# Layer 0 of a four-layer network: prelude in emitted order, its keys and first operand rows copied out of SBUF, transfers moved from GpSimd's queue to SyncE's

## The chip, the cores and the metric

One core of a Trainium2 chip runs the whole network in one launch. The metric is device time in microseconds (us); the times of several executions are given with their median. All data are float32. The core's engines are called as in the profile: PE (matrix multiplies), PEld (its weight loads), DVE (vector), ACT (scalar and activations), POOL (GpSimd), SP (which here only starts transfers, or DMAs). Each engine works through its own instructions in order, and one that waits holds up those behind it. DMAs can be started from SP, ACT or POOL.

## The reference

Four layers on an image of 2 x 64 x 64 positions with 128 channels. The change touches only layer 0, which is self-attention over the 4096 positions of each image with 4 heads of 32 channels and a learned relative bias in both directions:

```
x = x + L0(groupnorm(x))
q, k, v = split(x @ w_qkv)                    # 4 heads of 32
scores  = (q . k) / sqrt(32) + bias_w + bias_h   # [2, 4, 4096, 4096]
bias_w[query (x,y), key (a,b)] = q . pos_emb_w[b - y + 63]
bias_h[query (x,y), key (a,b)] = q . pos_emb_h[a - x + 63]
out     = softmax(scores) @ v
```

Layers 1 to 3 (a triangular product, an attention with a routed mixture of experts, and another such pair) follow it; their program does not change.

## The kernel before, in words

**Units, blocks and steps.** Layer 0 (function `layer0`) works on four *units*: image b and pair of heads p, in the order (0,0), (0,1), (1,0), (1,1). A unit has 8 *blocks* of 512 queries (`qb`), a block 4 *steps* (`xb`) of 1024 keys. So there are 32 blocks and 128 steps, written out in one loop by hand.

**A step.** For eight key tiles, PE makes scores `l0sc` (L766; four matmuls of 64 x 64 weights each, for two heads) into one of three PSUM buffers; ACT takes the exponential into an SBUF tile `l0es` (L774); DVE adds the tile into the running sum of the denominators `l0acc` (L777, L779). Then come a *piece* of side work (see below), and 32 matmuls `l0o` (L795) of the exponentials with the values. A step with `xb` 3 takes a second piece behind `l0o`.

**The bias inside the product.** A score matmul has 64 rows per head: 32 of q and k, 16 of the bias in one direction and 16 of that in the other. The keys' side is a tile `ka` (one for each pair p) whose lower rows hold keys and whose upper rows are constant one-hot rows, written on POOL by `l0_onehot` (L330). The queries' side is a tile `l0mv`, of which there are two, taken in turn by `xb % 2`. Function `fill` loads it over SP's queue: queries out of DRAM tensor `l0qd` (L629), rows of one bias out of `l0wd` (L632), rows of the other out of `l0hd` (L637). `prefill(at + 2)` at the end of a step starts the load for the step after the next one: 1 MB (`xb` 0 and 1, all three kinds), or 256 KB (`xb` 2 and 3, `l0hd` alone).

**How the bias rows are made** (`biases`, a generator of 17 pieces per unit). For each of 8 groups g: POOL turns the queries (`l0tq`, L567); PE multiplies them with the position table (`l0pw`, L539); ACT (or DVE) copies the result to a staging tile (`l0ew`, L550); two DMAs write it to DRAM (`l0sw`, L552); two DMAs read it back with a skewed pattern, which does the relative-to-absolute shift (`l0tw`, L586); POOL turns it back into its place (`l0rw`, L576). After eight groups four DMAs store `l0rw` as `l0wd` (L592). For the other direction (`l0ph`, `l0eh`, `l0sh`) the skewed read goes straight to `l0hd` (L598). The staging tile is one of the same ring of nine buffers as the exponentials (`tag="es", bufs=9`), so its DMA must have left it before its place is used again. `l0tw` has one buffer.

**Side work.** `side` is a list of generators, one piece of which is taken at each call of `piece()`: in unit 0 the rest of its own `biases`, those of unit 1, and the tokens (transposes and normalization) of image 1; in unit 1 the keys, values and queries of image 1 and the biases of unit 2; in unit 2 those of unit 3; in unit 3 none.

**Which queue.** Within the loop every DMA of the side work goes through `side_dma()`, which is POOL's queue there; SP's queue has only the fills and the copies of keys from DRAM into `ka` (`keys`, L615). Before the loop `side_dma()` is SP.

**End of a block.** While the next block runs: at its step 0 PE sums the denominators over partitions (`l0zb`, L700) and ACT copies them out; at step 1 DVE takes the reciprocal (L711) and POOL multiplies the numerators with it (`l0os`, L712); at step 2 PE folds the two halves (`l0po`, L717) and DVE adds the result to x (L728). `l0zb` and `l0po` share one PSUM buffer.

**Order.** The part ahead of the loop (the *prelude*: tokens, values, keys, queries of image 0, one-hot rows, and the first 11 pieces of unit 0's biases) is put in order by a scheduler. From `tc.manual_schedule()` on, which stands at the head of the loop, instructions are issued in the order in which the code emits them.

Of the kernel before, what the change touches and what calls it, by code (L numbers as in the profile page):

```python
# [14 lines left out]
P = 128  # L15
# [23 lines left out]
class Net:  # L39
# [239 lines left out]
    def l0_constants(self, wp, ap, ps, raw):  # L279

        nc = self.nc
        flip = ap.tile([P, 512], F32, tag="os", name="l0flip")[:, :P]
        nc.gpsimd.memset(flip, 0.0)
        nc.gpsimd.affine_select(
            out=flip,
            in_=flip,
            compare_op=ALU.not_equal,
            fill=1.0,
            base=2 - 2 * S,
            pattern=[[1, P]],  # L290
            channel_multiplier=1,
        )
        pos = wp.tile([P, 2, P], F32, tag="pos", name="l0pos")
        for i in range(2):
            pt = ps.tile([P, 512], F32, tag="misc", name=f"l0pe{i}")
            nc.tensor.matmul(
                pt[:, :P],
                lhsT=raw[:, i].rearrange("p h d -> p (h d)"),
                rhs=flip,
                start=True,  # L300
                stop=True,
            )
            nc.scalar.copy(pos[:, i, :], pt[:, :P])
        return pos
# [42 lines left out]
    def layer0(self):  # L347
# [7 lines left out]
        with ExitStack() as st:  # L355
            wp = st.enter_context(tc.tile_pool(name="l0w", bufs=1))
            ap = st.enter_context(tc.tile_pool(name="l0b", bufs=2))
            dp = st.enter_context(tc.tile_pool(name="l0d", bufs=1, space=DRAM))
            raw = self.l0_raw(ap)
            w = self.load(wp, "wqkv", [P, 3 * C], ins["L0_conv_w_qkv"])  # L360
# [12 lines left out]
            kd = [dp.tile([P, L], F32, tag=f"kd{b}", name=f"l0kd{b}") for b in range(B)]  # L373
# [9 lines left out]
            qTs, vs, rws = {}, {}, {}  # L383
# [12 lines left out]
            def side_dma():  # L396
                return nc.gpsimd if loop[0] else nc.sync

            def blocks(t, x):

                return t.rearrange("p (x a s k) -> p x s a k", x=NX, a=NX, s=2)[:, x]
# [10 lines left out]
            def tokens(ps, b):  # L412

                xT = ap.tile([P, L], F32, tag="xT", name=f"l0xT{b}", bufs=1)
                qTs[b] = xT
                st = self.small.tile([P, NC // 4, 6], F32, tag="gst", name=f"gst{b}", bufs=1)
                for x in range(NX):
                    pt = bank(ps, f"l0gt{b}_{x}")
                    for i in range(8):
                        nc.tensor.transpose(  # L420
                            pt[:, i // 4, i % 4 * P : (i % 4 + 1) * P],
                            self.x[:, b * NC + 8 * x + i, :],
                            self.ident,
                        )
                    for s in range(2):
                        nc.vector.bn_stats(st[:, 2 * x + s, :], pt[:, s, :])
                        nc.scalar.copy(
                            blocks(xT, x)[:, s].rearrange("p a (x y) -> p a x y", y=TB),
                            pt[:, s, :].rearrange("p (x a y) -> p a x y", a=NX, y=TB),
                        )  # L430
                    yield
                mv = self.small.tile([P, 2], F32, tag="gmv", name=f"gmv{b}")
                nc.vector.bn_aggr(mv, st)
                yield
                pm = bank(ps, f"gpm{b}")
                nc.tensor.matmul(
                    pm[:, 0, 0:1], lhsT=self.gmat, rhs=mv[:, 0:1], start=True, stop=True
                )
                gm = self.small.tile([P, 1], F32, tag="gm", name=f"gm{b}")
                nc.vector.tensor_copy(gm, pm[:, 0, 0:1])  # L440
                d = self.small.tile([P, 1], F32, tag="gd", name=f"gd{b}")
                nc.vector.tensor_tensor(d, mv[:, 0:1], gm, ALU.subtract)
                v = self.small.tile([P, 1], F32, tag="gv", name=f"gv{b}")
                nc.vector.scalar_tensor_tensor(v, d, d, mv[:, 1:2], ALU.mult, ALU.add)
                yield
                pv = bank(ps, f"gpv{b}")
                nc.tensor.matmul(pv[:, 0, 0:1], lhsT=self.gmat, rhs=v, start=True, stop=True)
                gr = self.small.tile([P, 1], F32, tag="gr", name=f"gr{b}")
                yield from self.rstd_parts(gr, pv[:, 0, 0:1], 1e-5, 1, apart=True)
                yield  # L450
                for x in range(NX):
                    part = xT[:, x * TB * S : (x + 1) * TB * S]
                    nc.vector.tensor_scalar(part, part, gm, gr, ALU.subtract, ALU.mult)
                    yield

            def project_v(ps, b):

                xT = qTs[b]
# [6 lines left out]
                for x in range(NX):  # L465
                    pv = bank(ps, f"l0pv{b}_{x}").rearrange("p s (i c) -> p (s i) c", c=C)
                    for i in range(8):
                        j = 8 * x + i
                        nc.tensor.matmul(
                            pv[:, i, :],  # L470
                            lhsT=xT[:, j * P : (j + 1) * P],
                            rhs=w[:, 2 * C :],
                            start=True,
                            stop=True,
                        )
# [9 lines left out]
            def project_k(ps, b):  # L485

                xT = qTs[b]
                for x in range(NX):
                    pk = bank(ps, f"l0pk{b}_{x}")
                    for s in range(2):  # L490
                        nc.tensor.matmul(
                            pk[:, s, :].rearrange("p (a k) -> p a k", k=P),
                            lhsT=w[:, C : 2 * C],
                            rhs=blocks(xT, x)[:, s],
                            start=True,
                            stop=True,
                        )
                    kst = staging(f"l0kst{b}_{x}")
                    nc.scalar.activation(kst, pk, AF.Copy, scale=root)
                    for s in range(2):  # L500
                        side_dma().dma_start(
                            out=blocks(kd[b], x)[:, s],
                            in_=kst[:, s, :].rearrange("p (a k) -> p a k", k=P),
                        )
                    yield

            def project_q(ps, b):

                xT = qTs[b]
                for x in range(NX):  # L510
                    pq = bank(ps, f"l0pq{b}_{x}")
                    for s in range(2):
# [3 lines left out]
                            rhs=blocks(xT, x)[:, s],  # L516
# [12 lines left out]
                    side_dma().dma_start(out=qd[b][:, cols], in_=xT[:, cols])  # L529
                    yield  # L530

            def slope(ps, u, n, g, tq):
# [16 lines left out]
                else:  # L549
                    nc.scalar.copy(ev[:LR], pt[:LR])  # L550
                for h in range(2):
                    side_dma().dma_start(  # L552
# [4 lines left out]
            def biases(hold, u):  # L557
# [15 lines left out]
                for k in range(2 * 8 + 1):  # L573
# [8 lines left out]
                    if 1 <= k < 9:  # L582
                        g = k - 1
                        tws[g] = ap.tile([P, 8, S], F32, tag="tw", name=f"l0tw{b}_{p}_{g}", bufs=1)
                        for h in range(2):
                            side_dma().dma_start(  # L586
# [3 lines left out]
                    if k == 9:  # L590
                        for c in range(0, L, L // 4):
                            side_dma().dma_start(  # L592
                                out=wd[u][:, c : c + L // 4], in_=rw[:, c : c + L // 4]
                            )
                    if k >= 9:
                        g = k - 9
                        for h in range(2):
                            side_dma().dma_start(  # L598
# [11 lines left out]
            def keys(u):  # L610
                b, p = u
                ka = kas[p]
                for h in range(2):
                    at = (2 * p + h) * HD
                    nc.sync.dma_start(  # L615
                        out=ka[64 * h : 64 * h + HD, :], in_=kd[b][at : at + HD, :]
# [6 lines left out]
            def fill(mv, u, qb, xb):  # L623
                b, p = u
                qs = slice(qb * 512, (qb + 1) * 512)
                for h in range(2):
                    at = (2 * p + h) * HD
                    if xb < 2:
                        nc.sync.dma_start(  # L629
                            out=mv[64 * h : 64 * h + HD], in_=wide(qd[b][at : at + HD, qs], HD)  # L630
                        )
                        nc.sync.dma_start(  # L632
                            out=mv[64 * h + 48 : 64 * h + 64],
                            in_=wd[u][:, qs].rearrange("(h s r) q -> h r s q", h=2, r=TB)[h],
                        )
# [6 lines left out]
            with tc.tile_pool(name="l0sp", bufs=2, space=PSUM) as ps:  # L642
# [3 lines left out]
                kas = self.l0_onehot(wp, ap, 2)  # L646
                for _ in project_v(ps, 0):
                    pass
# [4 lines left out]
                keys(units[0])  # L653
                hold = [ps]
                first[0] = biases(hold, units[0])
                for _ in range(11):
                    next(first[0])

            ps = st.enter_context(tc.tile_pool(name="l0p", bufs=1, space=PSUM))
            hold[0] = ps  # L660
            st.enter_context(tc.manual_schedule())
# [48 lines left out]
            def end_scale(e):  # L710
                nc.vector.reciprocal(e.r, e.r)  # L711
                nc.gpsimd.tensor_tensor(e.os, e.os, e.r, ALU.mult)  # L712
# [17 lines left out]
            mvs = [wp.tile([P, NX, 512], F32, tag=f"mv{i}", name=f"l0mv{i}") for i in range(2)]  # L730
# [10 lines left out]
            for at, (i, qb, xb) in enumerate(order):  # L741
# [3 lines left out]
                if (qb, xb) == (0, 1) and i == 0:  # L745
                    keys(units[1])
                if (qb, xb) == (7, 0) and i in (1, 2):
                    keys(units[i + 1])
# [33 lines left out]
                if prev:  # L782
# [4 lines left out]
                    elif xb == 2:  # L787
                        end_fold(prev)
# [16 lines left out]
            for part in (end_numerators, end_totals, end_scale, end_fold):  # L805
# [1292 lines left out]
```

## Time and profile before

| | |
|---|---|
| median of 3 runs | 4938.61 us (4929.92 to 4940.01) |
| the profiled execution | 4928.16 us |
| its span, first to last instruction | 4926.0 us |
| mean granted PE clock | 0.907 |
| first score matmul of the loop | 119.73 us after the start |
| last row of layer 0's end (addition to x) | about 1739 us |
| PE, DVE, ACT, POOL busy over the span | 88%, 62%, 48%, 20% |

The page of the profile gives each engine's busy time, the chain of work that ended last, and groups of instructions with their line, engine, count, mean time in ns and what ended the idle time before them. Besides, the trace can be asked for the waits in a stretch (who waited for whom, in total), for instructions in order of time ("start, duration, engine, line, ... [idle before <- what ended it]"), and for the busy time in stretches. POOLq and SPq are the queues' own instructions. The line numbers are those of the code above.

### The profile page before, as it was taken

What the parts mean: (1) busy time and instruction counts of PE and PEld (TensorE: products, weight loads), DVE (VectorE), ACT (ScalarE), POOL (GpSimd) and SP (SyncE); (2) the same over time, 40 slices, a digit from 0 to 9 for tenths busy, and PEclk for the clock granted to TensorE, in tenths of its full rate; (3) what the DMA queues carried; (4) which work ended last, traced back from release to release, by engine and by line L of the source; (5) the groups of instructions that cost most, each with busy time, mean ns of one, the idle gap of its engine ahead of it and who ended that gap; (6) DMA issues with size and microseconds to landing.
All of it is one profiled execution on the core that took longest, in us unless ns stands there. A gap on an engine that the chain in (4) does not pass through costs nothing.

```text
span 4926.0 us, 67757 instructions
## 1 busy us (share of the span) xinstructions
PE 4348.6 (88%) x27079; PEld 1851.4 (38%) x27079; DVE 3032.7 (62%) x4776; ACT 2377.9 (48%) x2850; POOL 991.0 (20%) x799
## 2 busy tenths in 40 slices
PE   4998999999999938488999999958999999999765
PEld 2222332323333326322332333328974444444432
DVE  2787887988999978646666565551043333333577
ACT  1666666666677614157777888820022222222200
POOL 4230023141000030134554555500020000000000
PEclk6999999999999958689999999965589999999889
DMA  5442334444333200000000000023300000000000
GB/s 161 97 112 56 73 81 106 85 108 84 66 58 63 46 8 1 25 1 1 1 1 1 1 1 1 1 71 103 103 2 0 0 0 0 0 0 0 6 13 22
DMA packets 150317, 192.25 MB, mean 39 GB/s; under 512 B 28996, under 2 KB 87204, under 8 KB 149602
## 3 DMA queue, kind: packets, MB, share of 16 engines
q1 hardware_dynamic: 113170, 130.34, 12.6%
q0 software_dynamic: 14912, 40.29, 2.8%
q10 hardware_dynamic: 21904, 17.12, 1.2%
q8 instruction: 218, 3.57, 0.3%
q14 instruction: 113, 0.93, 0.1%
HBM read 147.85 MB, written 48.23 MB: 40 GB/s over the span
## 4 chain that ended last, share of the span: by engine, by line
PE 60%; DVE 22%; ACT 5%; issue 5%; DMA 4%; POOL 3%; SPq 0%; DVEq 0%; ACTq 0%; POOLq 0%
DVE l0acc L779 10%; PE scl L1862 9%; PE oTl L1879 9%; PE l0sc L766 5%; PE l2sc L1491 5%; PE l2pos L1392 4%; PE l2av L1543 4%; PE l0o L795 3%; PE f3ex L2036 3%; PE f2po L1740 2%; PE f2ph L1714 2%; ACT l2es L1529 2%; DVE l0zs L711 1%; DMA l0sh<-l0eh 1%; DVE x L2044 1%
## 5 line engine op out<-in xcount | busy, mean ns | idle before, releaser
L779 DVE TENSOR_TENSOR l0acc<-l0acc,l0es 128x1024 f32<-128x1024 f32 x960 | 1221.3, 1272 | 175.0 <-ACT l0es L774 83.3
L774 ACT ACTIVATE l0es<-l0sc 128x1024 f32<-128x1024 f32 x1024 | 953.0, 1052 | 304.4 <-PE l0sc L766 284.6
L766 PE MATMUL l0sc<-l0mv,ka 64*64 64x512 f32 x8192 | 930.8, 601 | 74.7 <-DMA l0mv<-l0hd 40.6
L1887 DVE TENSOR_TENSOR accl<-accl,esl 128x1024 f32<-128x1024 f32 x240 | 294.0, 1225 | 540.8 <-ACT esl L1873 482.6
L1518 POOL TENSOR_TENSOR l2es<-l2es 128x1024 f32<-128x1024 f32 (+3 forms) x288 | 505.0, 1754 | 600.4 <-DVE l2es L1515 529.9
L766 PEld LDWEIGHTS l0sc<-l0mv,ka 64*64 64x64 f32 x8192 | 287.8, 133 | 710.3 <-ACT l0es L774 313.1
L1529 ACT ACTIVATE l2es<-l2es 128x1024 f32<-128x1024 f32 (+3 forms) x576 | 533.3, 977 | 6.9 <-POOL l2es L1522 6.7
L1873 ACT ACTIVATE esl<-scl 128x1024 f32<-128x1024 f32 x240 | 245.5, 1023 | 550.8 <-PE scl L1862 550.8
L1515 DVE TENSOR_SCALAR l2es<-l2sc 128x1024 f32<-128x1024 f32 (+3 forms) x272 | 306.4, 1126 | 294.7 <-PE l2sc L1491 292.1
L1862 PE MATMUL scl<-l3qT,l3kT 128*128 128x512 f32 x1024 | 484.2, 595 | 1.8 <-DVE bok_l L254 1.8
L795 PE MATMUL l0o<-l0es,l0v 128*32 128x512 f32 x4096 | 473.3, 603 | 0.0
L1879 PE MATMUL oTl<-esl,l3v 128*128 128x512 f32 x960 | 448.6, 592 | 0.0
L1505 ACT ACTIVATE l2es<-l2sc 128x1024 f32<-128x1024 f32 (+3 forms) x288 | 273.5, 950 | 257.8 <-PE l2sc L1491 254.5
L1491 PE MATMUL l2sc<-l2q,l2kT 32*128 32x512 f32 (+3 forms) x2304 | 339.4, 623 | 10.0 <-DVE l2es L1515 5.8
L1543 PE MATMUL l2av<-l2es,l2v 128*32 128x512 f32 (+3 forms) x2304 | 320.6, 577 | 8.9 <-ACT l2es L1529 8.8
L1392 PE MATMUL l2pos<-l2v,toe 128*32 128x512 f32 (+3 forms) x2304 | 297.9, 578 | 1.4 <-ACT l2v L1337 1.4
L1862 PEld LDWEIGHTS scl<-l3qT,l3kT 128*128 128x128 f32 x1024 | 193.0, 191 | 233.0 <-issue 218.4
L1879 PEld LDWEIGHTS oTl<-esl,l3v 128*128 128x128 f32 x960 | 182.5, 190 | 229.5 <-issue 225.6
L712 POOL TENSOR_TENSOR l0os<-l0os,l0zs 128x512 f32<-128x512 f32 x32 | 62.6, 1958 | 988.8 <-DVE l0zs L711 904.0
L795 PEld LDWEIGHTS l0o<-l0es,l0v 128*32 128x32 f32 x4096 | 122.9, 111 | 319.0 <-issue 317.3
L1491 PEld LDWEIGHTS l2sc<-l2q,l2kT 32*128 32x128 f32 x2304 | 100.5, 188 | 253.3 <-ACT l2es L1529 91.4
L2044 DVE SCALAR_TENSOR_TENSOR x<-f3ex,f3wt,x 128x128 f32<-128x128 f32 x512 | 160.1, 347 | 29.5 <-PE f3ex L2036 21.0
(457 smaller groups left out, 4335.9 us busy)
## 6 DMA issues: line engine op xcount, KB each, us to landing
l0mv<-l0qd SPq DMA_DIRECT2D x128, 256.0 KB
l0mv<-l0hd SPq DMA_DIRECT2D x256, 128.0 KB
l0mv<-l0wd SPq DMA_DIRECT2D x128, 128.0 KB
l0sh<-l0eh POOLq DMA_DIRECT2D x58, 144.0 KB, 5.2
f2w<-in_L_ffn_weight_dram ACTq DMA_DIRECT2D x32, 256.0 KB
f2w<-in_L_ffn_weight_dram ACTq DMA_DIRECT2D x8, 1024.0 KB
f2w<-in_L_ffn_weight_dram SPq DMA_DIRECT2D x8, 1024.0 KB
f2w<-in_L_ffn_weight_dram SPq DMA_DIRECT2D x32, 256.0 KB
```

The costliest lines, as they stand in the source:

```text
L766: nc.tensor.matmul(sc[64 * c : 64 * c + 64, h, :], lhsT=ka[rows, k0 : k0 + 64], rhs=mv[rows, NX - 1 - yb, :], start=True, stop=True,)
L774: nc.scalar.activation(es[yb, s], sc, AF.Exp)
L779: nc.vector.tensor_tensor(cur.acc, cur.acc, es[yb, s], ALU.add)
L795: nc.tensor.matmul(cur.o[lo : lo + HD, :], lhsT=v[:, 2 * (xb * NX + yb) + s, HD * h : HD * (h + 1)], rhs=es[yb, s][:, h, :], start=(xb == ...
L1392: nc.tensor.matmul(pos[c : c + 32, j0:, :], lhsT=toe[:, d * P + c : d * P + c + 32], rhs=v[:, n0 + j0 - d : n0 + 4 - d, :], start=(d == n0 ...
L1491: nc.tensor.matmul(sc[:, h2, off:], lhsT=kT[hs, cols], rhs=q[hs, off:], start=True, stop=True,)
L1515: nc.vector.tensor_scalar(es[:, :, lo:], sc[:, :, lo:], root, None, ALU.mult)
L1518: nc.gpsimd.tensor_tensor(part, part, part, ALU.mult)
L1529: nc.scalar.activation(e[:, :, off:], e[:, :, off:], AF.Silu)
L1543: nc.tensor.matmul(avs[i][hs, off:], lhsT=vs[b][:, k, hs], rhs=es[h // 2][:, h % 2, off:], start=(k == 0), stop=last,)
L1862: nc.tensor.matmul(sc[:, i, :], lhsT=kT[:, k * P : (k + 1) * P], rhs=qs, start=True, stop=True,)
L1879: nc.tensor.matmul(oT, lhsT=v[:, k, :], rhs=es[:, i, :], start=(k == 0), stop=(k == NC - 1),)
```

## The change

Six things are done in layer 0.

1. `tc.manual_schedule()` moves from the head of the loop to the head of the layer: the prelude is issued as emitted. In it the one-hot rows are emitted first, and the values last; the weights are loaded ahead of the position tables. The prelude's PSUM pool has four double buffers instead of two.
2. `side_dma()` goes: all side DMAs of the loop are started from SP. In the prelude the writes of `l0sw` and `l0sh` for even groups are started from ACT.
3. Image 0's normalized tokens are written to the two `l0mv` tiles, which are free then, and read from there by the projections. Keys are copied from the staging tile straight into `ka`; only those of unit (1,1) still go by DRAM (`kd`), and are fetched in unit 2's second step. The first unit's first block is filled from SBUF (`qTs`, `rws`) instead of from `l0qd` and `l0wd`.
4. In the prelude `l0tw` lies in two double tiles of the tag `acc`: four places instead of one.
5. The statistics are taken on the copied tokens in SBUF instead of on PSUM, and within the loop one piece later.
6. At a block's end the multiplication on POOL goes from step 1 to step 2, the fold from step 2 to step 3.

```
@@ layer0
+            st.enter_context(tc.manual_schedule())
+            w = self.load(wp, "wqkv", [P, 3 * C], ins["L0_conv_w_qkv"])
             raw = self.l0_raw(ap)
-            w = self.load(wp, "wqkv", [P, 3 * C], ins["L0_conv_w_qkv"])
...
+            mvs = [wp.tile([P, NX, 512], F32, tag=f"mv{i}", name=f"l0mv{i}") for i in range(2)]
+            kas = self.l0_onehot(wp, ap, 2)
...
-            def side_dma():
-                return nc.gpsimd if loop[0] else nc.sync
@@ tokens
-                        nc.vector.bn_stats(st[:, 2 * x + s, :], pt[:, s, :])
...
+                    if loop[0] and x:
+                        stats(x - 1)
+                    elif not loop[0]:
+                        stats(x)
@@ project_k
+                    for p in range(pairs):
+                        if (b, p) == (1, 1):
+                            nc.sync.dma_start(out=kd[:, cols], in_=kst[2 * HD :])
+                            continue
+                        for h in range(2):
+                            at = (2 * p + h) * HD
+                            nc.sync.dma_start(
+                                out=kas[p][64 * h : 64 * h + HD, cols], in_=kst[at : at + HD]
+                            )
@@ slope
+                queue = nc.sync if g % 2 or loop[0] else nc.scalar
                 for h in range(2):
-                    side_dma().dma_start(
+                    queue.dma_start(
@@ biases
-                        tws[g] = ap.tile([P, 8, S], F32, tag="tw", name=f"l0tw{b}_{p}_{g}", bufs=1)
+                        if loop[0]:
+                            tws[g] = ap.tile(
+                                [P, 8, S], F32, tag="tw", name=f"l0tw{b}_{p}_{g}", bufs=1
+                            )
+                        elif g % 2 == 0:
+                            tw2 = ap.tile(
+                                [P, 2, 8, S], F32, tag="acc", name=f"l0tw{b}_{p}_{g}"
+                            )
+                            tws[g], tws[g + 1] = tw2[:, 0], tw2[:, 1]
                         for h in range(2):
-                            side_dma().dma_start(
+                            nc.sync.dma_start(
@@ fill
+                        near = u == units[0] and qb == 0
+                        q = (qTs if near else qd)[b]
...
+                        if near:
+                            for s in range(NX):
+                                lo = 64 * h + TB * s
+                                nc.sync.dma_start(
+                                    out=mv[64 * h + 48 : 64 * h + 64, s],
+                                    in_=rws[u][lo : lo + TB, qs],
+                                )
@@ the prelude
-            with tc.tile_pool(name="l0sp", bufs=2, space=PSUM) as ps:
+            with tc.tile_pool(name="l0sp", bufs=4, space=PSUM) as ps:
                 for _ in tokens(ps, 0):
                     pass
                 pos = self.l0_constants(wp, ap, ps, raw)
-                kas = self.l0_onehot(wp, ap, 2)
-                for _ in project_v(ps, 0):
-                    pass
                 for _ in project_k(ps, 0):
...
                 for _ in range(11):
                     next(first[0])
+                for _ in project_v(ps, 0):
+                    pass
@@ the loop
             def end_scale(e):
                 nc.vector.reciprocal(e.r, e.r)
+
+            def end_mult(e):
                 nc.gpsimd.tensor_tensor(e.os, e.os, e.r, ALU.mult)
...
-                if (qb, xb) == (0, 1) and i == 0:
-                    keys(units[1])
-                if (qb, xb) == (7, 0) and i in (1, 2):
-                    keys(units[i + 1])
+                if (qb, xb) == (0, 1) and i == 2:
+                    keys()
...
                     elif xb == 2:
+                        end_mult(prev)
+                    else:
                         end_fold(prev)
```

## The prediction

> **What bounds the kernel now.** I read the page, then PE in order of time over layer 0, then the waits of the loop, then all engines at one stall, then the prelude.
>
> ```profile
> span 4926.0 us, 67757 instructions
> L779 DVE TENSOR_TENSOR l0acc<-l0acc,l0es 128x1024 f32<-128x1024 f32 x960 | 1221.3, 1272 | 175.0 <-ACT l0es L774 83.3
> ```
>
> Layer 0 ends near 1739 us; the other 3187 us don't change. DVE's additions are the costliest group. Whether they bound the loop is seen from the length of a block, the distance between two rows of `l0zb` (one per block):
>
> ```profile
> 776.64 1.07 PE L700 MATMUL l0zb<-l0acc,l0ones 128*32 128x512 f32 x8
> 837.71 1.07 PE L700 MATMUL l0zb<-l0acc,l0ones 128*32 128x512 f32 x8
> ...
> 1371.28 1.07 PE L700 MATMUL l0zb<-l0acc,l0ones 128*32 128x512 f32 x8
> 1416.32 1.07 PE L700 MATMUL l0zb<-l0acc,l0ones 128*32 128x512 f32 x8
> ```
>
> Block 12 takes 61.07 us, block 24, which has no side work, 45.04. Blocks 20 to 30 all take 45.03 to 45.05, and DVE has no gap in them:
>
> ```profile
> 1391.75 11.34 DVE L779 TENSOR_TENSOR l0acc<-l0acc,l0es 128x1024 f32<-128x1024 f32 x8
> 1403.01 0.42 DVE L728 TENSOR_TENSOR x<-x,l0po 128x256 f32<-128x256 f32 x1
> 1403.34 10.52 DVE L779 TENSOR_TENSOR l0acc<-l0acc,l0es 128x1024 f32<-128x1024 f32 x8
> ```
>
> So a quiet block is DVE's: 45.04. PE needs 4 x (7.03 scores + 3.57 values) + 0.9 + 1.0 = 44.3 for one. A block with five slope matmuls of 1.03 needs 49.5 of PE, yet takes 54 to 62. What fills the rest is in the loop's waits (119 to 1765 us; total, times, longest):
>
> ```profile
> POOL l0hd L598 <- DMA l0sh<-l0eh: 100.8, 29, 8.1
> ...
> ACT l0eh L550 <- DMA l0sh<-l0eh: 45.6, 9, 13.3
> ...
> ACT l0ew L550 <- DMA l0sw<-l0ew: 40.2, 5, 10.9
> ...
> PE l0po L717 <- POOL l0os L712: 20.6, 17, 5.6
> ...
> PE l0pw L539 <- POOL l0tq L567: 19.4, 5, 11.4
> ```
>
> A slope's write to DRAM lands in a median 5.2 us, a step is 11.6 us long, and still ACT waits up to 13.3 for one. The stall in block 12 says why (POOL, ACT, PE in order of time):
>
> ```profile
> 798.77 2.13 POOL L712 TENSOR_TENSOR l0os<-l0os,l0zs 128x512 f32<-128x512 f32 x1 [12.45 <-DVE l0zs L711]
> ...
> 807.63 1.10 POOL L552 DMA_DIRECT2D l0sh<-l0eh  x2
> ...
> 816.62 1.01 ACT L550 COPY l0eh<-l0ph 72x1024 f32<-72x1024 f32 x1 [13.28 <-DMA l0sh<-l0eh]
> ...
> 817.68 7.26 PE L766 MATMUL l0sc<-l0mv,ka 64*64 64x512 f32 x48 [8.93 <-ACT l0eh L550]
> ```
>
> The write of a slope copied at 791 us starts only at 807.63: in POOL's queue it stood behind a multiplication that waited 12.45 us for DVE's reciprocal, behind a turning copy and behind other DMAs. Its staging tile stayed taken, ACT stopped, PE's three score buffers filled, PE stopped for 8.93.
>
> The prelude (0 to 119.73) is a chain:
>
> ```profile
> 2.57 30.46 POOL L330 TENSOR_TENSOR ka<-l0rev 32x1024 f32<-32x1024 f32 x16
> ...
> 27.89 1.39 DVE L442 TENSOR_TENSOR gd<-gmv,gm 128x1 f32<-128x1 f32 x1
> 29.31 1.85 DVE L444 SCALAR_TENSOR_TENSOR gv<-gd,gmv 128x1 f32<-128x1 f32 x1
> ...
> 77.35 1.06 POOL l0rw L576
> 78.44 0.58 SPq L586
> 79.06 3.16 DMA l0tw<-l0sw
> ```
>
> With one place for `l0tw`, each of eight groups waits for the copy before it: 4.8 us each, from 72.5 to 106.9.
>
> **The change, part by part.**
>
> *Transfers to SP, multiplication a step later (parts 2 and 6 of the change).* POOL keeps `l0tq`, `l0rw` and `l0os`; SP waits for landings instead. Blocks would fall to the larger of PE's 44.3 + 1.03 per slope and DVE's 45.04 + 1.3 for each pair of turning copies beside it (eight additions beside such a pair took 11.87 us at 759 us, 10.53 without). By groups, from the rows of `l0zb`:
> - 1, 2, 11, 16 (mostly width slopes; four or five pairs, DVE's): 231.3 now, 4 x 50.2 then: 30.5 gained.
> - 3, 12, 17, 18 (height slopes, PE's 49.5): 224.4 now, 198 then: 26.4.
> - 13, 19: 95.0 now, 93 then: 2.
> - 4 to 7 (last slopes, tokens of image 1): 211.2 now. DVE needs 4 x 45.04 + 5.5 of statistics + 3.1 of normalizing + 2 of small ones = 191. The later statistics take them out of ACT's way, but chains through PE stay: I take 197, so 14.
> - 8 to 10 (keys, values, queries; 160.1) have PE busy throughout already; 14, 15 and 20 to 31 are DVE's: 0. There the move of the fold only turns PE's 0.68 us wait at `l0po` into one at `l0zb`.
>
> Sum 73. DMA issue on POOL (0.55 to 0.76 each, 236 of them in the loop) isn't on the path by itself and counts 0.
>
> *What it adds: SP now waits too, and the fills stand behind it.* A step's SP order is: skewed read (waits for the last slope's landing), slope write (waits for ACT's copy), fill. A full fill is 1 MB; in the quiet stretch 1349 to 1360 us such a one kept the DMA engines at a share of 0.59 of 11 us, 6.5 us, so I estimate 8.5 from first issue to landing. It has from the end of a step's scores to the start of the step after next: 14.2 us quiet, 16 with a slope in each step. With one piece SP gets to it 3 us late: 3 + 8.5 + 2 for 0.5 MB ahead of it fits. With two pieces (`xb` 3, and the fill then is always a full one) the second skewed read waits for the write just issued: fold, slope and copy 3.1, two issues 1.2, landing 2.7 (prelude, 63.89 to 66.62), two reads 1.2, two writes 1.1: the fill starts 9.3 late and lands at 19 to 20; needed at 18.7. About ten such steps: bounds 0 and 3 each, taken 1: 10. The 2 MB of `l0wd` go into the same queue: unit 3's ahead of a full fill, about 5 us once. Loss 15, so the loop gains 58 (bounds 35 to 78).
>
> Here a rule speaks against the change: the Trainium skill ("DMA: Bandwidth & Descriptors", section "Issuing engines are not separate DMA queues") has all issuers end on the same 16 DMA engines, so that another issuer saves only issue time. By it the loop would gain about nothing. But the row at 807.63 shows 15.5 us lost between the copy and the issue, not in the transfer; I take the row.
>
> *The prelude.* Values (PE 34.53 to 44.30) leave the head of the chain. But in emitted order POOL does all one-hot rows first and the flip matrix after them, and `l0pe`, which needs it, stands ahead of the keys on PE. One-hot rows end at 33.0 now. Four normalizing instructions (0.75 each) will now fall beside them, near 23 us. The Trainium skill ("SBUF — State Buffer", "Who interferes with whom") has DVE and POOL share a port pair under an exclusive lock, which two-input operations and fast one-input ones take; the trace agrees for the first kind (1.39 and 1.85 us for one column beside the one-hot rows, where other such rows have 0.16), and shows none of the second. By the lock POOL loses 3 us, without it 0: I take 3. So keys start at 37.3 and, as PE is then cold (the first values took 3.8 us for eight, later ones 1.8), lose 2.8: 4.2 ahead of now. Next, `l0tq` 3 now stands behind `l0rw` 0 on POOL, and odd writes behind the wait of a read on SP. Following each group (copy 1.05, matmul 1.7, copy 1.1, write landing 2.7, read landing 3.9), pairs come every 8 us or less and the last `l0rw` ends 39.3 us after the first `l0tq` starts, 47.2 now: 7.9 gained. Behind it SP has `l0wd` (4 issues, 2.9), two reads, write and landing of `l0sh` 1 (4 to 5 in all), two reads, then 12 small issues (5.2) and the landing: 18 us to a full `l0mv`, against 15.5 now (106.9 to 122.4): 2.5 lost. The values' matmuls (about 10) lie beside the `l0tw` chain, ready before the fill needs their `l0mv`; 12 DMA issues on ACT, about 7 us, lie where ACT is idle for 43. Fewer DMAs for queries and no wait for `l0kd`: 0, SP is not late there. Prelude: 9.6 gained (bounds -5 to 20).
>
> Sum: 58 + 9.6 = 68. Against the profiled execution, 4928.2 - 68 = 4860; that one stands 10.4 under the median of the runs, so the median becomes 4938.6 - 68 = 4871.
>
> **The rivals.**
> - *POOL and DVE take it back.* Width blocks come out at 45.04 + 5 x 1.3 = 51.5, late fills at 2 us, and the emitted order gains nothing in the prelude (-5): 73 - 5 - 25 - 5 = 38, so 4900. For it: DVE without gap in quiet blocks. Against: DVE idles 2 to 12 us per slope block now.
> - *SP takes POOL's place.* The same head-of-line wait, now ahead of the fills that every step needs: PE would stop at `l0sc <- DMA l0mv`. It decides the sign when it costs 83 us over 53 slope pieces, 1.6 us each beyond the slack. At 2.5 each: 132 - 83 = 49 slower, 4988. Against: single pieces have 2 us or more of slack by the count above.
> - *Nothing shown.* The DMAs themselves are late, whoever issues them, as the rule has it; the prelude's 10 remain or not: 4934.
>
> **How the numbers follow.** Forecast 0.62 (4871, own range 4838 to 4908), first rival 0.20 (4900), SP 0.11 (4988), nothing 0.07 (4934). The range 4835 to 4925 leaves out SP's case, the last and the ends of the others. About 0.2%, 10 us, is what a measurement can tell from no change. Faster by more: 0.62 + 0.20 + 0.03 = 0.85; within: 0.05; slower: 0.10.
>
> **What would show it.** Right: rows of `l0zb` 49.5 to 51 apart in slope blocks, no `ACT l0eh <- DMA` above 2 us, quiet blocks still 45.04, first scores near 110 us, the wait at `l0po` gone. Wrong: `PE l0sc <- DMA l0mv` of several us in steps behind two pieces (SP); slope blocks at 54 or more with ACT waiting for `l0sh` as now (nothing); keys starting after 40 us, or more than 42 us from first `l0tq` to last `l0rw` (prelude).

## The result and the profile after

The changed kernel takes 4870.51 us in the median of four runs (4857.27 to 4876.00), the kernel before 4939.31 in the median of four (4929.92 to 4946.82): a ratio of 0.9858, 95% interval 0.9831 to 0.9884. The forecast was 4871. The profiled execution took 4876.00 us, 52.2 less than that of before.

The same lines of the page as before, with the line numbers of the changed code:

```profile
span 4873.4 us, 67788 instructions
L819 DVE TENSOR_TENSOR l0acc<-l0acc,l0es 128x1024 f32<-128x1024 f32 x960 | 1225.4, 1276 | 131.5 <-ACT l0es L814 36.3
```

DVE's additions cost the same, but the time it waited for exponentials ahead of them fell from 83.3 to 36.3 us. PE in order of time gives the length of block 12, which was 61.07:

```profile
687.69 1.07 PE L741 MATMUL l0zb<-l0acc,l0ones 128*32 128x512 f32 x8
737.39 1.06 PE L741 MATMUL l0zb<-l0acc,l0ones 128*32 128x512 f32 x8
```

It is 49.70 now. The waits of the loop (119 to 1765 us; total, times, longest):

```profile
PE l0zb L741 <- DVE x L771: 20.0, 14, 7.9
...
PE l0sc L806 <- DMA l0mv<-l0hd: 7.0, 4, 3.0
...
PE l0po L760 <- POOL l0os L755: 5.7, 1, 5.7
...
ACT l0eh L578 <- DMA l0sh<-l0eh: 2.4, 1, 2.4
...
PE l0pw L567 <- POOL l0tq L596: 0.7, 1, 0.7
```

ACT's waits for a slope's staging tile, 45.6 and 40.2 us before, are down to 2.4; PE's waits for the turned queries from 19.4 to 0.7 and for the multiplication from 20.6 to 5.7, which is the one wait behind the last block. In the quiet blocks PE waits at `l0zb` for DVE's addition to x, as forecast, but at a small price: a block of 45.04 has become one of 45.24, and the last block 45.26 instead of 42.64.

Layer 0 ends at 1678.86 us (end of the last addition to x) and ended at 1738.96: 60.1 less. Nearly all of it is the loop: from the first row of `l0zb` to the last it takes 1490.4 us instead of 1550.0. The prelude gave 0.7: the first `l0zb` row stands at 178.44, before at 179.18.

The rest of the program, the same code in all kernels here, took 3187.0 us in the profiled execution of before, 3194.5 in that of after, and between 3168.0 and 3198.4 over the profiled executions of the ten kernels told of here. That spread is half of what is looked for. So the experiments below are read first by where layer 0 ends, and the run times stand beside it.

### The profile page after: what moved, and what is told of

Read it like the earlier page. It is cut to its first block, busy times and chain, and to the rows that moved or that the text cites. A ratio compares the mean times of both kernels' runs of the same rounds, so it can differ in the third digit from the quotient of the medians.

```text
span 4873.4 us, 67788 instructions
## 1 busy us (share of the span) xinstructions
PE 4343.6 (89%) x27079; PEld 1864.5 (38%) x27079; DVE 3046.7 (63%) x4776; ACT 2380.1 (49%) x2850; POOL 856.4 (18%) x561
## 4 chain that ended last, share of the span: by engine, by line
PE 68%; DVE 21%; ACT 4%; issue 3%; DMA 2%; POOL 1%; SPq 0%; DVEq 0%; ACTq 0%; POOLq 0%
PE l0sc L806 11%; DVE l0acc L819 10%; PE scl L1904 9%; PE oTl L1921 9%; PE l0o L837 5%; PE l2sc L1533 5%; PE l2pos L1434 4%; PE l2av L1585 4%; PE f3ex L2078 3%; PE f2po L1782 2%; PE f2ph L1756 2%; ACT l2es L1571 2%; DVE x L2086 1%; PE l2pu L1418 1%; DVE l2es L1557 1%
## 5 line engine op out<-in xcount | busy, mean ns | idle before, releaser
L819 DVE TENSOR_TENSOR l0acc<-l0acc,l0es 128x1024 f32<-128x1024 f32 x960 | 1225.4, 1276 | 131.5 <-ACT l0es L814 36.3
L1915 ACT ACTIVATE esl<-scl 128x1024 f32<-128x1024 f32 x240 | 245.8, 1024 | 550.5 <-PE scl L1904 550.5
L2086 DVE SCALAR_TENSOR_TENSOR x<-f3ex,f3wt,x 128x128 f32<-128x128 f32 x512 | 160.1, 347 | 28.5 <-PE f3ex L2078 20.0
```

The source lines that it names most:

```text
L819: nc.vector.tensor_tensor(cur.acc, cur.acc, es[yb, s], ALU.add)
```

## Experiments on the loop

My theory was the forecast's: the transfers' queue and the multiplication share one cause, POOL's order, and either cure alone brings much of the gain. The rival was that one of the two does it and the other nothing or harm. Four kernels make a square of the two parts: before with the transfers on SP (`q_sp`), before with the multiplication a step later (`mult_only`), after with the transfers back on POOL (`q_pool`), after with the multiplication back at step 1 (`mult_back`).

**`q_sp`, the queue alone.**

```
             def side_dma():
-                return nc.gpsimd if loop[0] else nc.sync
+                return nc.sync
```

> The kernel before with one edit: in the loop the side DMAs start from SP's queue instead of POOL's. Theory 1 (POOL's queue order was the loss): slope blocks fall from 54 to 62 us to about 50, first to last l0zb row from 1550.0 us to 1495 to 1508, layer 0 ends 42 to 55 us earlier, time 4939 to about 4890. Rival (the later multiplication does most of it): less than 20 us gained, since l0tq still waits behind l0os on POOL. Rival (SP's waits eat it): gain under 10 and a wait of PE for l0mv behind every second piece.

**`mult_only`, the multiplication alone.**

```
             def end_scale(e):
                 nc.vector.reciprocal(e.r, e.r)
+
+            def end_mult(e):
                 nc.gpsimd.tensor_tensor(e.os, e.os, e.r, ALU.mult)
...
                     elif xb == 2:
+                        end_mult(prev)
+                    else:
                         end_fold(prev)
```

> The kernel before with one edit: the multiplication on POOL a step later, the fold two steps after the reciprocal. Theory 1: POOL no longer stands 12 us in front of a reciprocal with DMAs behind it, so a part of the stalls goes, 10 to 25 us of layer 0; the DMAs' waits for landings on POOL's queue stay. Rival (the multiplication does most of it): 45 us or more. Quiet blocks stay at 45.0 to 45.3 in both.

**`q_pool`, the change with the loop's transfers on POOL.**

```
-                queue = nc.sync if g % 2 or loop[0] else nc.scalar
+                queue = nc.gpsimd if loop[0] else nc.sync if g % 2 else nc.scalar
...
-                            nc.sync.dma_start(
+                            side_dma().dma_start(
                                 out=tws[g][S * h
```

with the same edit for the other side transfers (`kd`, `qd`, `ka` in the loop, `wd`, `hd`).

> The changed kernel with the loop's side DMAs back on POOL's queue, all else kept. Theory 1: most of the loop's gain goes: first to last l0zb row from 1490.4 back to 1525 to 1545 us, time about 4870 + 40. Rival (the multiplication does most of it): 1500 or less, time within 10 us of the changed kernel's.

**`mult_back`, the change with the multiplication at step 1 and the fold at step 2.**

```
-                    elif xb == 2:
-                        end_mult(prev)
-                    else:
+                    elif xb == 2:
                         end_fold(prev)
```

with the multiplication again behind the reciprocal in `end_scale`.

> The changed kernel with the multiplication back at step 1 and the fold at step 2. Theory 1: loses 5 to 15 us: waits of PE for l0os and, through POOL's order, for l0tq. Rival (the multiplication does most of the gain): loses 35 us or more. Quiet blocks 45.04 as before the change instead of 45.25.

Measured, with the profiled executions' times of layer 0 and groups of blocks as in the forecast (block i lies between rows i - 1 and i of `l0zb`, counted from 0; summed):

| | before | q_sp | mult_back | mult_only | after | q_pool |
|---|---|---|---|---|---|---|
| transfers in the loop on | POOL | SP | SP | POOL | SP | POOL |
| multiplication at step | 1 | 1 | 1 | 2 | 2 | 2 |
| parts 1, 3, 4, 5 | no | no | yes | no | yes | yes |
| end of layer 0, us | 1738.96 | 1718.12 | 1714.46 | 1685.98 | 1678.86 | 1668.90 |
| loop, first to last `l0zb` | 1550.0 | 1530.2 | 1526.2 | 1496.9 | 1490.4 | 1482.7 |
| blocks 1, 2, 11, 16 | 231.3 | 223.9 | 223.7 | 198.7 | 200.2 | 197.7 |
| blocks 3, 12, 17, 18 | 224.4 | 216.0 | 218.8 | 209.6 | 207.1 | 205.3 |
| blocks 4 to 7 | 211.2 | 208.8 | 201.9 | 202.6 | 196.8 | 195.3 |
| blocks 8 to 10 | 160.1 | 160.1 | 160.3 | 162.3 | 162.5 | 160.8 |

Run times, against 4930.03 for before, measured beside them (10 runs): `q_sp` 4902.56, ratio 0.9950 (0.9933 to 0.9966); `mult_back` 4895.22, 0.9936 (0.9920 to 0.9953); `mult_only` 4885.09, 0.9906 (0.9890 to 0.9923); `q_pool` 4865.57, 0.9877 (0.9861 to 0.9894).

The theory fell; the rival's figures came true, but for `q_sp`, which gained 20.8 where under 20 was expected. The multiplication alone takes 53.0 us off layer 0, 88% of what the whole change takes; put back in the change, it costs 35.6. The queue alone takes those 20.8. Once the multiplication has moved, no gain from the queue is seen: the change with its transfers back on POOL ends layer 0 10.0 us *earlier* than the change itself, 7.7 of it in the loop. The run times do not part these two (the ratios' intervals overlap), and further below kernels with one and the same loop differ by up to 7.5 us in it, so which of the two queues is then the better is not shown.

What the queue alone leaves is seen in the waits of `q_sp` (119 to 1765 us):

```profile
PE l0po L717 <- POOL l0os L712: 20.9, 18, 5.7
...
PE l0pw L539 <- POOL l0tq L567: 19.7, 5, 11.4
...
ACT l0ew L550 <- DMA l0sw<-l0ew: 13.9, 3, 5.1
...
ACT l0eh L550 <- DMA l0sh<-l0eh: 10.0, 1, 10.0
```

ACT's two waits fell from 85.8 to 23.9 in sum, so the transfers do get away earlier. But the two waits for POOL's own results are as long as before, 20.9 and 19.7. `mult_back` has the same two, 20.9 and 19.7. In order of time, block 1 of `q_sp` shows which instruction is in the way (POOL, then PE):

```profile
199.38 1.26 POOL L712 TENSOR_TENSOR l0os<-l0os,l0zs 128x512 f32<-128x512 f32 x1 [94.11 <-DVE l0zs L711]
200.58 2.00 POOL L567 COPY l0tq<-l0xT 128x512 f32<-128x512 f32 x2
```

```profile
201.66 1.98 PE L539 MATMUL l0pw<-l0tq,l0pos 32*72 32x512 f32 x4 [11.36 <-POOL l0tq L567]
```

POOL had nothing else to do and stood at the head of its queue for the reciprocal; the turning copy behind it was ready, and PE lost 11.36 us for it. No choice of queue for the DMAs cures that.

Even the stall of block 12, which the forecast explained by POOL's queue, is still there in `q_sp`: the block takes 59.70 us, before 61.07, in `mult_only` 49.70. POOL's multiplication starts at 791.37 after waiting 24.78, the last `l0rw` is copied behind it until 795.46, and SP, whose next DMA in order is the `l0wd` made of it, gets to the slope's write at 800.91 and to a fill at 802.04. PE then waits for that fill:

```profile
806.54 10.04 PE L766 MATMUL l0sc<-l0mv,ka 64*64 64x512 f32 x64 [6.99 <-DMA l0mv<-l0hd]
```

On either queue the DMA stood behind the multiplication, on SP by way of `l0rw`.

A step later, the multiplication waits too, but what the step needs has gone ahead of it. POOL of the changed kernel, block 12:

```profile
692.35 1.16 POOL L605 COPY l0rw<-l0tw 128x512 f32<-128x512 f32 x1 [6.22 <-DMA l0tw<-l0sw]
693.36 2.01 POOL L596 COPY l0tq<-l0xT 128x512 f32<-128x512 f32 x1
709.43 2.06 POOL L755 TENSOR_TENSOR l0os<-l0os,l0zs 128x512 f32<-128x512 f32 x1 [14.06 <-DVE l0zs L752]
```

It waits 14.06 us, longer than the 12.45 of the stall in the kernel before, and PE has no wait for it: step 1's `l0rw` and `l0tq` stand ahead of it.

The transfers on POOL keep waits that SP doesn't have. Those of `mult_only`:

```profile
ACT l0eh L550 <- DMA l0sh<-l0eh: 20.8, 4, 9.4
...
ACT l0ew L550 <- DMA l0sw<-l0ew: 8.8, 2, 4.8
```

29.6 us where the change has 2.4. On ACT, which has slack, most of them cost little: the loop of `q_pool`, whose two are 16.7 and 8.9, is the shortest of the six. What SP has in their place are waits of PE for fills. The changed kernel in block 18, PE and then SP:

```profile
1032.67 1.07 PE L806 MATMUL l0sc<-l0mv,ka 64*64 64x512 f32 x4 [3.00 <-DMA l0mv<-l0hd]
1034.89 10.06 PE L806 MATMUL l0sc<-l0mv,ka 64*64 64x512 f32 x60 [1.15 <-DMA l0mv<-l0hd]
```

```profile
1018.98 2.76 SPq L629 DMA_DIRECT2D l0wd<-l0rw  x4
1021.84 2.46 SPq L635 DMA_DIRECT2D l0hd<-l0sh  x2
1024.35 1.07 SPq L581 DMA_DIRECT2D l0sh<-l0eh  x2
1025.53 0.33 SPq L665 DMA_DIRECT2D l0mv<-l0qd  x1
```

The first fill of the next step starts behind the 2 MB of `l0wd`, a skewed read and a write, and PE waits for it. Block 18 takes 57.95 us; a slope block bound by PE takes 49.7, so 8.3 are lost in this one place: 4.2 in the two waits, and most of the rest in the 60 matmuls behind, which take 10.06 us where 64 took 7.10 a step later: the granted PE clock was 0.50 from 1035 to 1040 us, after five microseconds in which PE worked for 1.18. But this loss is not SP's alone. On POOL's queue block 18 takes 55.05 (`q_pool`) and 57.13 (`mult_only`), and there PE waits too, for ACT, whose staging tile is late (`q_pool`, then `mult_only`):

```profile
1028.39 6.71 PE L809 MATMUL l0sc<-l0mv,ka 64*64 64x512 f32 x48 [3.79 <-ACT l0eh L581]
...
1044.76 7.45 PE L768 MATMUL l0sc<-l0mv,ka 64*64 64x512 f32 x48 [5.15 <-ACT l0eh L550]
```

In all three the 2 MB of `l0wd` are issued just before; in the changed kernel the DMA engines' busy share is 0.99 from 1024 to 1035 us. That full DMA engines are the cause is argued from this and was not tested by a run.

## Experiments on the prelude

The prelude was to give 9.6 us and gave 0.7. Its rows in the changed kernel, POOL, DVE and PE in order of time:

```profile
2.06 32.16 POOL L330 TENSOR_TENSOR ka<-l0rev 32x1024 f32<-32x1024 f32 x16
...
23.05 9.38 DVE L474 TENSOR_SCALAR l0mv<-l0xT,gm,gr 128x1024 f32<-128x1024 f32 x4
...
34.90 1.22 PE L296 MATMUL l0pe<-l0flip,l0raw 128*128 128x128 f32 x4 [16.91 <-POOL l0flip L284]
...
35.91 9.47 PE L509 MATMUL l0pk<-l0mv,wqkv 128*128 128x512 f32 x16
```

PE waits 16.91 us for the flip matrix behind POOL's one-hot rows, as forecast, and the keys start at 35.91. Then SP (the last line is SP's own entry in the list of waits, 38 to 100 us):

```profile
40.62 19.81 SPq L530 DMA_DIRECT2D ka<-l0kst  x16
60.86 4.23 SPq L557 DMA_DIRECT2D l0qd<-l0xT  x4
66.65 1.35 SPq L623 DMA_DIRECT2D l0tw<-l0sw  x2
```

```profile
SPq L530 <- DMA l0sw<-l0ew: 9.8, 1, 9.8
```

The sixteenth copy of keys waits 9.8 us for ACT's first write of a slope, which has no data in common with it. The first skewed read therefore starts at 66.65 us; in the kernel before it started at 66.62. All that the earlier keys had gained is gone there. The reason is a completion semaphore, the counter that a DMA raises when it lands. In the trace's records of the program all DMAs of SP and ACT use the same eight semaphores (101 to 106, 108, 109), POOL's eight others. The sixteenth copy waits for semaphore 101 and then uses it itself, and the last to use it was the write that ACT had started at 57.86. The rival, that the DMA engines had no room, doesn't fit: their busy share is 0.00 from 52 to 58 us, while SP waits. The next two kernels test it.

**`slopes_sp`:** the writes of all slopes from SP again, none from ACT.

```
-                queue = nc.sync if g % 2 or loop[0] else nc.scalar
+                queue = nc.sync
```

> The changed kernel with the prelude's even slope writes on SP's queue again, so that no DMA of SP shares a completion semaphore with one of ACT's. Theory (SP's 16th key copy waited 9.8 us for ACT's first slope write, with which it shares one of eight completion semaphores): that copy starts by 52 instead of 59.92 us, the first l0tw read by 61 instead of 66.65; but all writes and reads are in one order then, some 4.5 us per group, so the last l0rw ends at 96 to 100 instead of 100.7, layer 0 ends 1 to 5 us earlier. Rival (the DMA engines were full, so the copy had to wait): it starts at 59 to 60 as now.

**`keys_pool`:** image 0's keys of the second pair of heads from POOL, so that SP has eight copies.

```
-                            nc.sync.dma_start(
+                            (nc.gpsimd if p else nc.sync).dma_start(
                                 out=kas[p][64 * h : 64 * h + HD, cols], in_=kst[at : at + HD]
```

> The changed kernel with image 0's keys of the second pair copied from POOL's queue, idle then, instead of SP's. Theory (a wait by a shared semaphore): the first l0tw read starts at about 60 instead of 66.65, last l0rw ends near 95, first scores about 5 us earlier than 117.57. Rival (DMA engines full): no change over 1 us.

**`flip_first`:** the flip matrix on POOL ahead of the one-hot rows.

```
+            flip = self.l0_flip(ap)
             kas = self.l0_onehot(wp, ap, 2)
...
-                pos = self.l0_constants(wp, ap, ps, raw)
+                pos = self.l0_constants(wp, ap, ps, raw, flip)
```

> The changed kernel with the flip matrix made on POOL ahead of the one-hot rows. Theory: the keys no longer wait for POOL but for the normalized tokens, which stay slow beside the one-hot rows (9.4 us for four); keys start near 26 instead of 35.91, queries end near 42 instead of 52.3, and the whole prelude is 7 to 10 us shorter. Rival (the key copies on SP and its semaphores set the start of the l0tw chain): 3 us or less.

**`best2`:** the change with `flip_first`, `keys_pool`, the loop's transfers on POOL as in `q_pool`, and in the prelude `l0tq` ahead of `l0rw` on POOL:

```
+                    if k < 7 and not loop[0]:
+                        turned_q(k + 1)
                     if 2 <= k < 10:
                         g = k - 2
                         nc.gpsimd.tensor_copy(
...
-                    if k < 7:
+                    if k < 7 and loop[0]:
                         turned_q(k + 1)
```

> The changed kernel with the loop's side DMAs back on POOL's queue, and in the prelude the flip matrix first, the second pair's keys copied from POOL's queue and l0tq ahead of l0rw in POOL's order. If the loop's gain is the multiplication's and the prelude's loss is made of these waits: last score sum (l0zb 31) about 1640 instead of 1668.8 us, layer 0 ends 25 to 32 us earlier than in the changed kernel, time near 4845. If they aren't additive, 10 to 15 us earlier.

| | before | after | slopes_sp | keys_pool | flip_first | best2 |
|---|---|---|---|---|---|---|
| first skewed read, us | 66.62 | 66.65 | 58.45 | 58.12 | 55.87 | 48.88 |
| first scores | 119.73 | 117.57 | 110.96 | 109.12 | 105.72 | 94.89 |
| first `l0zb` | 179.18 | 178.44 | 171.25 | 169.83 | 166.76 | 154.90 |
| loop | 1550.0 | 1490.4 | 1486.4 | 1486.9 | 1491.0 | 1490.2 |
| end of layer 0 | 1738.96 | 1678.86 | 1667.65 | 1666.77 | 1667.77 | 1655.17 |

Run times, against 4937.29 for before, measured beside them (9 runs): `slopes_sp` 4853.54, ratio 0.9817 (0.9801 to 0.9834); `keys_pool` 4859.45, 0.9824 (0.9804 to 0.9845); `flip_first` 4862.52, 0.9834 (0.9816 to 0.9852); `best2` 4839.72 (5 runs), 0.9800 (0.9783 to 0.9817). All four gained in the direction expected. The sizes were off: the first three took 11 to 12 us off layer 0, where 1 to 5 was expected of `slopes_sp`, first scores about 5 earlier of `keys_pool` (8.5) and a prelude 7 to 10 shorter of `flip_first` (11.9); of `best2`, 25 to 32 was expected and it took 23.7.

In `slopes_sp` no DMA is started from ACT in the prelude, and the wait is gone. SP in order of time:

```profile
50.87 3.06 SPq L557 DMA_DIRECT2D l0qd<-l0xT  x4
56.41 0.76 SPq L581 DMA_DIRECT2D l0sw<-l0ew  x2
58.45 1.43 SPq L623 DMA_DIRECT2D l0tw<-l0sw  x2
```

The key copies are through at 50.8, and the first read comes 8.2 us earlier though SP now starts more DMAs itself. `keys_pool` leaves ACT's writes where they are and gets there too, at 58.12. Two different edits that take the two DMAs off one semaphore take the wait away; with the records above that shows it. Starting the writes from ACT, the part of the change that was to relieve SP, is what held SP up.

`flip_first` takes away the other wait, PE's for the flip matrix. PE in order of time:

```profile
26.00 9.06 PE L515 MATMUL l0pk<-l0mv,wqkv 128*128 128x512 f32 x16 [4.98 <-DVE l0mv L480]
34.89 7.03 PE L547 MATMUL l0pq<-l0mv,wqkv 128*128 128x512 f32 x16
```

Keys start at 26.00 instead of 35.91, as soon as DVE has normalized the first quarter. SP's key copies are still 18.58 us long in it (30.71 to 49.29): the false wait remains and moves along, and the first scores come 11.9 earlier.

`best2` starts the loop's scores 22.7 us ahead of the change and ends layer 0 23.7 ahead. Its ratio lies below those of all others measured, but its interval touches those of the other three measured with it; it beats the kernel before by 1.8 to 2.2%. Its loop is 1490.2, not the 1482.7 of `q_pool`, though the loop's code is the same; the four kernels with the change's loop lie between 1486.4 and 1491.0. Of the 7.5 between `q_pool` and `best2`, 2.2 are in the quiet blocks and the rest in small parts in blocks 2 to 5, 8 and 18. Why a shorter prelude makes the loop longer wasn't tried and stays open.

## Why the prediction was right, and where its steps were wrong

**The loop: the sum right, the cause put to the wrong part.** Forecast 58 (73 less 15), measured 59.6. The stall was read rightly: a multiplication that waits for the reciprocal at the head of POOL's queue. The step that failed is "transfers to SP, multiplication a step later" as one entry with one price. The row at 807.63 showed a DMA stuck behind the multiplication, and I took it that either move would free it; on SP the same write came no sooner, since `l0wd` ahead of it needs POOL's `l0rw` (block 12 of `q_sp`, above). And the same forecast quoted PE's waits for `l0os` (20.6) and for `l0tq` (19.4): those are POOL's own results, which only the multiplication's move frees. Split by those lines, the working would have said that the queue alone leaves 40 us of PE's waits where they are, and so it did (20.9 + 19.7 in `q_sp`).

By groups, forecast and measured: blocks 1, 2, 11 and 16: 200.8 and 200.2. Blocks 13 and 19: 93 and 92.9. Blocks 4 to 7: 197 and 196.8; of that gain the moved multiplication has 8.6 (`mult_only`, 202.6), and block 4, 56.2 before, is at 48.7 to 48.8 in all three kernels with parts 3 to 5 and at 55.5 in `q_sp` and `mult_only`. That fits the later statistics, which were not run alone. Blocks 3, 12, 17 and 18: 198 and 207.1, the one miss: block 18's 57.95, with blocks 3, 12 and 17 at 49.7 to 49.8 where 49.5 was forecast. Blocks 8 to 10: no change forecast, 2.4 lost; quiet blocks: none forecast, 2.9 lost over all 14, nearly all of it in the last one (2.6).

**What SP would cost.** Forecast 15: ten fills behind two pieces, late by 1 us each, and 5 once for `l0wd` ahead of a full fill. The late fills hardly exist: PE's waits for fills are four in the whole loop, 7.0 us. The single one was under-sized: 8.3, not 5; and it is only in part SP's, since on POOL's queue the same block lost 5.4 and 7.4. With the 2.4 and 2.9 just named the loss is 13.6, so its size came out for other reasons than those given: the groups gained 31.1, 17.3, 2.1 and 14.4, with block 18's 8.3 already taken off, and 64.9 - 2.4 - 2.9 = 59.6.

**The rule that was set aside.** The Trainium skill ("DMA: Bandwidth & Descriptors", section "Issuing engines are not separate DMA queues") has another issuer save only issue time. I weighed it against the 15.5 us between copy and issue and took the row. The runs put it in between. With the multiplication at step 1 another queue is worth 20.8 us of layer 0, since the issue was stuck in an engine's order, of which the rule doesn't speak. With that cause gone, `q_pool` against the change shows no gain from SP, as the rule says. The row was right, and what I built on it was too much.

**The prelude: forecast 9.6, measured 0.7 to the first `l0zb` and 1.0 to a full `l0mv` (122.42 and 121.44).** First scores came at 117.57, not near 110, and the forecast's own sign of a wrong prelude, more than 42 us from the first `l0tq` to the last `l0rw`, came true. By stretches: 6.0 gained to the first `l0tq` (forecast 4.2), 0.2 in the chain behind it (7.9), 5.2 lost from there to a full `l0mv` (2.5). The steps in turn:
- Keys at 37.3, measured 35.91. Right.
- PE cold, 2.8 lost: the keys' sixteen matmuls took 9.47 us, the queries' sixteen behind them 7.03, so 2.4; the granted clock was 0.52 from 36 to 41 us and 1.00 after that. Right.
- POOL 3 us longer by the shared port: 32.16 against 30.46, 1.7; DVE paid the greater part (below). Only POOL's part counted: the flip matrix, made behind POOL's rows, came last, and DVE was done at 32.4.
- "Fewer DMAs for queries and no wait for `l0kd`: 0, SP is not late there." This is the step that failed. SP was late by 9.8 us, by a wait that no row of before could show, because ACT started no slope's DMA there. It was costed at nothing without naming what covers it.
- First `l0tq` to last `l0rw` 39.3: measured 47.0 (53.70 to 100.71), against 47.2 before. So four places for `l0tw` brought nothing while SP was late. Here `l0tq` 3 behind `l0rw` 0 was priced too low:

```profile
70.92 1.04 POOL L605 COPY l0rw<-l0tw 128x512 f32<-128x512 f32 x1 [12.94 <-DMA l0tw<-l0sw]
...
72.91 1.98 PE L567 MATMUL l0pw<-l0tq,l0pos 32*72 32x512 f32 x4 [12.72 <-POOL l0tq L596]
```

  POOL waits 12.94 us for the first skewed read and PE 12.72 for the turning copy behind that, though its queries had long been there. In `best2`, with `l0tq` first and SP unhindered, the same chain takes 33.0 (43.55 to 76.53).
- 18 us from the last `l0rw` to a full `l0mv`: 20.7, since fills from SBUF took up to 0.65 us an issue where 0.43 was taken.

**The total.** 68 forecast, 60.1 measured in layer 0, and 68.8 between the medians of the runs. That the medians agree is luck: layer 0 fell short by 8, nearly all in the prelude, and if layer 0 takes the same in every run, the other 8.7 are scatter of the rest of the program, whose code did not change.

**The rivals.** "POOL and DVE take it back" was nearer in the prelude and wrong of the loop: width blocks are at 50, not 51.5, and fills are not late. "SP takes POOL's place" was there in kind, with 7.0 us of PE's waits on fills instead of 132. "Nothing shown" was wrong of the whole, and of the queue alone, which gave 20.8; it holds of the queue only once the multiplication has moved.

## What to carry to other kernels

When two edits cure the same stall, list the waits that each of them can end and price them apart: an in-order engine that stands at a wait delays its results as well as its DMAs, and changing the DMAs' queue helps only the latter. Move the waiting instruction behind the work that others need first, even if it then waits longer. A DMA given to a second queue can still hold up the first through a completion semaphore that the compiled program shares between them, so a changed issuer is checked by the first transfers behind it, not only by its own issue time.

## What the runs showed of the hardware

- Four normalizations of 1024 columns on DVE take 2.98 us alone (33.47 in the kernel before) and 9.38 beside POOL's one-hot rows (9.39 in `flip_first` and `best2`), while POOL's sixteen rows grow only from 30.46 to 32.16. The Trainium skill ("SBUF — State Buffer", section "Who interferes with whom") tells of the exclusive lock on the port pair and of tensor-scalar operations taking it. The trace agrees that the two hold each other up; I had let POOL pay 3 us, and DVE paid 6.4, POOL at most 1.7.
- The same program behind layer 0 took 3168.0 to 3198.4 us from one profiled execution to another. Where a part of a program is changed, a mark at the end of that part is free of this spread; here it rests on one profile of each kernel.
